# A transformer kernel: the engines' orders, the PSUM banks and the splitting of maxima are changed

## The chip, the cores and the metric

The kernel runs on one core of a Trainium2 chip. The metric is device time in microseconds (us) from the start to the end of one execution; the runs of the kernel before took 1797.16 to 1802.51 us, with a median of 1798.53 us. A core has five engines that run side by side, each through its own instructions in a fixed order: TensorE (PE, matrix products into PSUM), VectorE (DVE), ScalarE (ACT), GpSimd (POOL) and SyncE (SP, which here only starts DMAs). An instruction that needs another engine's result waits for a semaphore, and what stands behind it on its engine waits too. PSUM has eight banks, each of which holds 512 float32 values on each of 128 partitions.

## The reference

The input x has 16 sequences of 512 tokens with 128 values. Two layers follow each other, all in float32:

```python
x = x + attn0(layernorm(x))   # 16 heads of 8, softmax(q k^T / sqrt(8)) v, output projection
x = x + ffn0(layernorm(x))    # silu(x Wg) * (x Wu), then Wd; 384 hidden values, integer weights / 127
x = x + attn1(layernorm(x))   # as attn0, with q and k normalised per head (rms_norm) and weighted
x = x + ffn1(layernorm(x))    # base_w, plus 8 low-rank experts weighted by a softmax router
```

The softmax subtracts each row's maximum before the exponential, and so does the kernel. For each sequence and layer there are 16 heads x 512 queries x 512 keys of scores.

## The kernel before

One sequence in one layer is a unit; there are 32 units, and `units` lists them so that a sequence's second layer comes at least six units after its first (LAG). A unit has four phases.

- `pre(n)`: layer norm (bn_stats on DVE, the rest on POOL), transposes on PE, projections to q and k. `split_stack` (L205) writes each of q and k as a sum of three bf16 parts (ACT and POOL) and starts 24 DMAs on SP (L232) that stack the parts into `qst` and `kst`, so that one bf16 matmul of about 61 rows gives a score of float32 precision. Three sets of these stacks exist (NST).
- Maxima: `max_tile` (L336) multiplies for 128 queries and 512 keys (L343); DVE reduces the 512 columns to the negative maximum (L350). Two heads use the upper and lower 64 rows of PE and run together as a pair. After half a unit `split_max` (L354) splits the maxima into three bf16 parts on DVE, and `put_max` (L363) brings them through PE (L368) and ACT (L376) and with two DMAs on ACT's queue (L378) into three more rows of `qst`. The next product then has its row maximum subtracted.
- Exponentials and values: a step is one (n, i, kc); there are 16 in a unit, 512 in all. `exp_pair` makes two pairs of transposed scores in a step (L395) and ACT takes their exponentials (L403). `values` (L405) multiplies four heads at once by v and a column of ones (L415), in one PSUM bank of its own. After four steps ACT copies the bank (L425) and starts a DMA to DRAM (L427).
- `gather(n)` fetches the sums and the denominators from DRAM in another layout (L452 to L458), and `post(n)` has the output projection and the feed-forward part.

Everything but the values takes its PSUM bank from one pool `psw` of seven banks that go round. The order of PE and POOL is written out by hand: `attend(s)` issues one step after `ORDER = "0mmvmm1b"` (a pair of scores, a pair of maxima, values, a pair of maxima, a pair of scores, other work), and the generators `pre`, `gather` and `post` are advanced at fixed steps after the tables PRE, POST and GATHER (`plan`, `agenda`). The maxima run LEAD = 13 steps ahead of the exponentials. DVE, ACT and SP are ordered by the framework's own scheduler.

Of the kernel before, what the change touches and what calls it, by code (L numbers as in the profile page):

```python
# [17 lines left out]
DRAM = bass.MemoryType.DRAM  # L18

P = 128  # L20
S = 512
# [9 lines left out]
LOWEST = -3.4028234e38  # L31
# [13 lines left out]


LAG = 6
LEAD = 13
LEAD0 = 13
PUT = 2  # L50
ORDER = "0mmvmm1b"
PRE = (
    (-4, 4, 8, 20, 21, 21),
    (1, 2, 4, 6, 7, 9, 9, 12, 12, 12, 14, 20, 21, 22),
)
POST = (
    (5, 7, 9, 10, 11, 12, 13, 15, 15, 16, 17, 17, 17, 17),
    (5, 7, 8, 8, 9, 11, 12, 13),
)
GATHER = (1, 1, 3)  # L60
# [3 lines left out]
BO0, BQK1, BP1, BB1, RB1, REND = 0, 128, 384, 512, 640, 648  # L64


@with_exitstack
def encoder_kernel(ctx: ExitStack, tc: tile.TileContext, x, wf, wi, lb, cols, rows, out):
# [4 lines left out]
    xp = ctx.enter_context(tc.tile_pool(name="xp", bufs=LAG + 3))  # L73
    p1 = ctx.enter_context(tc.tile_pool(name="p1", bufs=1))
    p2 = ctx.enter_context(tc.tile_pool(name="p2", bufs=2))
    pp = ctx.enter_context(tc.tile_pool(name="pp", bufs=3))
    dr = ctx.enter_context(tc.tile_pool(name="dr", bufs=2, space=DRAM))
    psw = ctx.enter_context(tc.tile_pool(name="psw", bufs=7, space=PSUM))
    psa = ctx.enter_context(tc.tile_pool(name="psa", bufs=1, space=PSUM))

    xt_of = {}

    def load_x(b):
        xt = xp.tile([P, C, P], F32, tag="xt", name=f"xt{b}")
        nc.sync.dma_start(xt, x[b].rearrange("(c p) d -> p c d", p=P))
        xt_of[b] = xt
# [29 lines left out]
    def fill(i):  # L116

        eng = nc.vector if i == 0 else nc.gpsimd
        eng.memset(kst[i].rearrange("p t s -> p (t s)").bitcast(F32), ONES)
        eng.memset(vst[i], 1.0)  # L120

    def fill_q(i):

        q = qst[i].rearrange("p t s -> p (t s)").bitcast(F32)
        if i == 0:
            nc.scalar.activation(q, zero[:, None, :].to_broadcast([P, 4, S]), AF.Copy)
        else:
            nc.gpsimd.memset(q, 0.0)

    def weights():  # L130

        for layer, (lo, bb) in enumerate(((WO0, BO0), (WP1, BP1))):
            bvb = p1.tile([P, P], F32, tag="bvb", name=f"bvb{layer}")
            nc.vector.tensor_scalar(bvb, zero[:, :P], cl[:, 4 + layer : 5 + layer], None, ALU.add)
            ps = psw.tile([P, P], F32, tag="w", name=f"bvp{layer}")
            nc.tensor.matmul(ps, bvb, w[:, lo : lo + P], start=True, stop=True)
            nc.vector.tensor_tensor(row[:, bb : bb + P], row[:, bb : bb + P], ps, ALU.add)
            yield
        nc.vector.tensor_copy(identb, ident)
        nc.vector.tensor_scalar(b2, b2, 2.0, None, ALU.mult)  # L140
        nc.vector.tensor_scalar(qkn, cl[:, 2:4], math.sqrt(HD), None, ALU.mult)
        yield
        for k in range(3):
            wint = p1.tile([P, HID], I32, tag="wint", name=f"wint{k}")
            nc.scalar.dma_start(wint, wi[:, k * HID : (k + 1) * HID])
            if k < 2:
                nc.vector.tensor_copy(wgu[:, k * HID : (k + 1) * HID], wint)
            else:
                nc.vector.tensor_scalar(
                    wd.rearrange("p f o -> p (f o)"), wint, 0.5 / 127.0**3, None, ALU.mult  # L150
                )
            yield

    fill(0)
    fill_q(0)
# [9 lines left out]
    )  # L165
    av_last = [None]

    av_of, nm_of, num_of, mp_of, p_of, acc_of = ({} for _ in range(6))

    def layer_norm(xt, nm, alone=False):  # L170
        st = p2.tile([P, C, 6], F32, tag="st", name=f"st{nm}")
# [621 lines left out]
```

## Time and profile before

| | |
|---|---|
| profiled execution, its time | 1800.01 us |
| its span, first to last instruction | 1798.0 us |
| median of three runs | 1798.53 us |
| mean granted TensorE clock | 0.976 |
| POOL busy | 753.8 us (42%) |
| SP: stack DMAs issued | 768, 64 KB each, 0.61 us of SP for most |
| ACT: DMAs issued | 127 of 256 KB (0.33 us each), 128 of 12 KB (0.73 us each) |

How to read what follows: a row of a group gives line, engine, operation, output<-input, shapes and the count; then the busy time in us and the mean of one in ns; then the idle time of the engine just before these instructions and what ended most of it. Matmuls are pipelined: a row of 0.39 us for a pair doesn't mean that the next pair starts 0.39 us later, so the distance between the starts is used here. A float32 matmul is recorded twice. In a timeline the columns are start and duration in us, and brackets show the idle time before. In a tile view the columns are the shortest, median and longest duration in ns and the first and last start in us.

### The profile page before, as it was taken

Reading aid. Unit: us, or ns where it says so; the run is one execution under the profiler, and the core shown is the slowest. Engines: PE = TensorE matmul, PEld = TensorE weight load, DVE = VectorE, ACT = ScalarE, POOL = GpSimd, SP = SyncE. Lnnn points to the kernel's source line nnn. Section 1 sums busy time; section 2 is a strip of 40 time slices with the busy share of each in tenths; the row PEclk is TensorE's granted clock in tenths of the full one; section 3 lists DMA queues with packets and bytes.
Section 4 is the critical chain, followed back from the end, with each engine's and each line's share of the span. In section 5 each row is a group of like instructions: output and inputs, shape, how many; then the busy total and the mean of one; then the engine's idle time right before and its main releaser. Section 6 shows DMA issues by size and latency. Waiting matters only on the chain.

```text
span 1798.0 us, 30523 instructions
## 1 busy us (share of the span) xinstructions
PE 1676.6 (93%) x10574; PEld 552.3 (31%) x10574; DVE 1577.7 (88%) x3234; ACT 1346.7 (75%) x2578; POOL 753.8 (42%) x853
## 2 busy tenths in 40 slices
PE   4899999999999999999999999999999999998996
PEld 1223233322323223233323323323232333332323
DVE  6888989899898998989899998989998999998973
ACT  2388868878787777878878787887877877787783
POOL 4223345344354345345345444434445555454111
PEclk7699999999999999999999999999999999999997
DMA  5332232232332223233232342323233123333110
GB/s 124 41 73 63 60 67 50 62 62 60 68 75 56 72 62 72 68 67 68 58 71 67 61 82 55 70 63 63 64 74 70 49 68 60 67 73 73 45 45 27
DMA packets 111658, 115.85 MB, mean 64 GB/s; under 512 B 19300, under 2 KB 86852, under 8 KB 111504
## 3 DMA queue, kind: packets, MB, share of 16 engines
q1 hardware_dynamic: 90612, 77.64, 23.4%
q10 hardware_dynamic: 20892, 36.26, 5.7%
q8 instruction: 83, 1.36, 0.3%
q14 instruction: 71, 0.58, 0.1%
HBM read 23.43 MB, written 38.53 MB: 34 GB/s over the span
## 4 chain that ended last, share of the span: by engine, by line
PE 55%; DVE 27%; DMA 11%; ACT 2%; issue 2%; SPq 1%; POOL 1%; ACTq 0%; POOLq 0%; DVEq 0%
PE avp L415 19%; DVE nm L350 19%; PE s L343 11%; PE st L395 6%; DMA qst<-a10a 4%; PE u_f L513 3%; PE g_f L507 3%; PE d_f L526 2%; ACT p L403 2%; PE r_f L589 1%; PE r_f L588 1%; PE o L480 1%; DMA dav<-av 1%; PE pm L368 1%; DMA kst<-a31a 1%
## 5 line engine op out<-in xcount | busy, mean ns | idle before, releaser
L350 DVE TENSOR_REDUCE nm<-s 128x1 f32<-128x512 f32 x2048 | 1296.4, 681 | 148.8 <-PE s L343 141.2
L403 ACT ACTIVATE p<-st 128x512 f32<-128x512 f32 x2048 | 1091.9, 599 | 325.3 <-PE st L395 266.3
L415 PE MATMUL avp<-p,vst 128*32 128x512 f32 x4096 | 629.0, 606 | 21.3 <-ACT p L403 21.3
L343 PE MATMUL s<-kst,qst 61*128 61x512 bf16 x2048 | 490.7, 388 | 56.2 <-DVE nm L350 20.8
L395 PE MATMUL st<-qst,kst 64*128 64x512 bf16 x2048 | 371.9, 381 | 2.1 <-DMA qst<-msb 2.0
L343 PEld LDWEIGHTS <-qst 61*128 61x128 bf16 x2048 | 115.9, 94 | 508.3 <-issue 479.0
L415 PEld LDWEIGHTS avp<-p,vst 128*32 128x32 f32 x4096 | 112.0, 108 | 367.1 <-issue 234.4
L460 POOL TENSOR_TENSOR num<-num,rdb 128x512 f32<-128x512 f32 x31 | 39.5, 1273 | 306.2 <-DMA rdb<-drd 306.2
L395 PEld LDWEIGHTS <-kst 64*128 64x128 bf16 x2048 | 104.8, 95 | 136.1 <-issue 94.8
L519 POOL TENSOR_TENSOR h_f<-th_f,ub_f 128x512 f32<-128x512 f32 x32 | 40.9, 1277 | 237.8 <-ACT ub_f L518 237.8
L220 POOL TENSOR_TENSOR t1a<-t1a,a11a 128x512 f32<-128x512 f32 x31 | 36.0, 1162 | 161.5 <-ACT a11a L214 116.1
L425 ACT ACTIVATE av<-avp 128x512 f32<-128x512 f32 x128 | 76.5, 598 | 19.3 <-PE avp L415 16.9
L567 POOL TENSOR_TENSOR cf_f<-gt_f,mid_f 128x256 f32<-128x256 bf16 x16 | 9.9, 620 | 128.7 <-DVE gt_f L565 128.7
L201 POOL TENSOR_TENSOR xt<-xt,row 128x512 f32<-128x512 f32 x48 | 61.6, 1283 | 2.7 <-DVE xna L184 1.4
L376 ACT ACTIVATE msb<-pm 24x512 bf16<-24x512 f32 x64 | 36.8, 574 | 29.6 <-PE pm L368 29.6
L513 PE MATMUL u_f<-xTf,wgu 128*128 128x512 f32 x96 | 54.0, 645 | 0.0
L507 PE MATMUL g_f<-xTf,wgu 128*128 128x512 f32 x96 | 52.3, 627 | 0.0
L526 PE MATMUL d_f<-wd,h_f 128*128 128x128 f32 x384 | 47.1, 279 | 0.0
L526 PEld LDWEIGHTS d_f<-wd,h_f 128*128 128x128 f32 x384 | 44.1, 192 | 6.8 <-issue 5.1
L220 POOL TENSOR_TENSOR t0a<-t0a,a10a 128x512 f32<-128x512 f32 x31 | 35.9, 1159 | 16.7 <-ACT a10a L214 13.0
L224 POOL TENSOR_TENSOR a20a<-t0a,zero 128x512 bf16<-128x512 f32 x31 | 39.6, 1277 | 2.4
L297 POOL TENSOR_TENSOR qksa<-qksa,ria 128x512 f32<-128x512 f32 x32 | 40.0, 1271 | 1.2
(140 smaller groups left out, 1633.9 us busy)
## 6 DMA issues: line engine op xcount, KB each, us to landing
dav<-av ACTq DMA_DIRECT2D x127, 256.0 KB
kst<-a11a SPq DMA_DIRECT2D x192, 64.0 KB
qst<-a10a SPq DMA_DIRECT2D x192, 64.0 KB
kst<-a21a SPq DMA_DIRECT2D x128, 64.0 KB
qst<-a20a SPq DMA_DIRECT2D x128, 64.0 KB
num<-dav SPq DMA_DIRECT2D x31, 256.0 KB
rdb<-drd SPq DMA_DIRECT2D x31, 256.0 KB
xt<-in_x_dram SPq DMA_DIRECT2D x16, 256.0 KB
```

The costliest lines, as they stand in the source:

```text
L201: nc.gpsimd.tensor_tensor(xt, xt, row[:, None, lo : lo + P].to_broadcast([P, C, P]), ALU.add)
L220: eng.tensor_tensor(t, t, a1, ALU.subtract)
L343: nc.tensor.matmul(ps, qst[n % NST][band, t, qc * P : (qc + 1) * P], kst[n % NST][band, t], start=True, stop=True,)
L350: nc.vector.tensor_reduce(nm_of[n, hf][:, qc, half, t % 4 : t % 4 + 1], ps, AX.X, ALU.max, negate=True)
L395: nc.tensor.matmul(st[half], kst[n % NST][band, t, kc * P : (kc + 1) * P], qst[n % NST][band, t], start=True, stop=True,)
L403: nc.scalar.activation(p_of[n, i, kc][:, 2 * jp + half], st[half], AF.Exp, scale=SCALE)
L415: nc.tensor.matmul(acc[32 * j : 32 * j + 32], vst[n % NST][:, kc, lo : lo + 32], pt[:, j], start=(kc == 0), stop=(kc == C - 1), tile_posit ...
L425: nc.scalar.activation(av, acc, AF.Copy)
L507: nc.tensor.matmul(pg, wgu[:, f * P : (f + 1) * P], xT, start=True, stop=True)
L513: nc.tensor.matmul(pu, wgu[:, HID + f * P : HID + (f + 1) * P], xT, start=True, stop=True)
L519: nc.gpsimd.tensor_tensor(h[:, f], th, ub, ALU.mult)
L526: nc.tensor.matmul(ps[:, c], h[:, f, c * P : (c + 1) * P], wd[:, f], start=(f == 0), stop=(f == NF - 1),)
```

## The change

- A class `Plan` in the kernel now orders all five engines. Every piece of work is a generator that yields (engine, estimated ns, priority, kind, what it waits for). `Plan.run` keeps one estimated clock per engine, picks the piece that can start first (among those within EPS the one of lowest priority), and adds estimates for the way between engines (START, TAIL). For PE `choose` goes through PATTERN, where m is a pair of maxima, e a pair of scores, v values and w other work. What comes out is a fixed order; at run time the engines still wait for semaphores.
- The eight PSUM banks are allocated once and handed out by `Banks`: three for maxima, three for scores, one for all other work, and one for the values as before. A pair is planned when two banks of its kind are free.
- The splitting of the maxima (four small operations for each half unit) moves from DVE to POOL, inside `put_max`.
- The DMAs of the values (L427) and of the maxima (L378) move from ACT's queue to SP, so SP starts all DMAs. The stack DMAs are ordered by part.
- The exponentials' SBUF tiles are eight of two heads instead of three of four; LEAD is 20, as a priority only; the integer weights are loaded from SP.

The core of the diff:

```diff
-LEAD = 13
-PUT = 2
-ORDER = "0mmvmm1b"
+LEAD = 20
+NP = 8
+VLAG = 2.0
+EPS = {"PE": 40, "ACT": 100, "DVE": 150, "POOL": 100, "SP": 0}
+PATTERN = "mevmew"
+TOL = {"m": 400, "e": 400, "v": 200, "w": 200}
+NB_M, NB_E = 3, 3
...
+START = {"PE": 45, "ACT": 22, "DVE": 22, "POOL": 68, "SP": 25}
+TAIL = {"PE": 185, "ACT": 118, "DVE": 98, "POOL": 20, "SP": 2600}
+SWITCH = 100
+def act(n, ptr=0):
+    return 51 + n / 1.2 + 93 * ptr
+def red(n):
+    return 62 + n / 0.96
...
-    psw = ctx.enter_context(tc.tile_pool(name="psw", bufs=7, space=PSUM))
-    psa = ctx.enter_context(tc.tile_pool(name="psa", bufs=1, space=PSUM))
+    pst = [ps.tile([P, S], F32, tag=f"ps{k}", name=f"ps{k}") for k in range(8)]
+    acc = pst[7]
+    mbanks = Banks(pst[:NB_M])
+    ebanks = Banks(pst[NB_M : NB_M + NB_E])
+    banks = Banks(pst[NB_M + NB_E : 7])
...
+                    pr = 16 * n + 8 * hf + j / 2 - LEAD
+                    waits = [mbanks.two, ("q", n), ("k", n)]
+                    e = yield "PE", 220, pr, "m", waits
...
-        nc.vector.tensor_copy(mp[:, :, :, 0], nm)
-        nc.vector.tensor_tensor(r1, nm, mp[:, :, :, 0], ALU.subtract)
-        nc.vector.tensor_copy(mp[:, :, :, 1], r1)
-        nc.vector.tensor_tensor(mp[:, :, :, 2], r1, mp[:, :, :, 1], ALU.subtract)
+            t = yield "POOL", 310, pr, None, waits
+                nc.gpsimd.tensor_copy(mp[:, :, :, 0], nm)
+                nc.gpsimd.tensor_tensor(r1, nm, mp[:, :, :, 0], ALU.subtract)
+                nc.gpsimd.tensor_copy(mp[:, :, :, 1], r1)
+                nc.gpsimd.tensor_tensor(mp[:, :, :, 2], r1, mp[:, :, :, 1], ALU.subtract)
...
-            nc.scalar.dma_start(
-                Q[half * HP + MROW : (half + 1) * HP, 4 * hf : 4 * hf + 4],
+            e = yield "SP", 60, pr + 1, None, (t,)
+            nc.sync.dma_start(
+                qst[n % NST][half * HP + MROW : (half + 1) * HP, 4 * hf : 4 * hf + 4],
...
-                nc.scalar.dma_start(av_of[n][i], av)
+            e = yield "SP", 60, pr, None, (t,), 800
+            nc.sync.dma_start(av_of[n][i], av)
...
-    with tc.manual_schedule(engines={mybir.EngineType.PE, mybir.EngineType.Pool}):
-        for s in range(min(agenda), max(agenda) + 1):
-            attend(s)
-        flush()
+    plan.spawn(weights())
+    for i in range(1, NST):
+        plan.spawn(fill(i))
+    plan.spawn(scores())
+    plan.spawn(values())
+    plan.spawn(maxima())
+    for n in range(NU):
+        plan.spawn(chain(n))
+    with tc.manual_schedule(engines={ET.PE, ET.Pool, ET.DVE, ET.Activation, ET.SP}):
+        plan.run()
```

In the changed kernel the maxima's matmul is L625, their reduction L640, the splitting L656 to L663, `put_max`'s matmul L669 and its DMAs L682, the scores L704, the exponentials L721, the values L738.

## The prediction, made before the changed kernel had run

> **What bounds the kernel now.** I read the page's engine shares first, then the costliest groups, the waits, two stretches of the timeline, and last the tiles qst and msb.
>
> ```profile
> PE 1676.6 (93%) x10574; PEld 552.3 (31%) x10574; DVE 1577.7 (88%) x3234; ACT 1346.7 (75%) x2578; POOL 753.8 (42%) x853
> ...
> L350 DVE TENSOR_REDUCE nm<-s 128x1 f32<-128x512 f32 x2048 | 1296.4, 681 | 148.8 <-PE s L343 141.2
> L403 ACT ACTIVATE p<-st 128x512 f32<-128x512 f32 x2048 | 1091.9, 599 | 325.3 <-PE st L395 266.3
> ```
>
> Two engines look full, and each waits for the other: VectorE (DVE) has 141.2 us of idle time that a score matmul of the maxima (L343) ended. One step is one (n, i, kc) of the exponentials; there are 512. The tile view of qst and, under it, the timeline of TensorE (PE) give the period and its parts.
>
> ```profile
> L395 PE MATMUL st<-qst,kst x2048: 372/378/632, 70.5 to 1769.0; 64*128 64x512 bf16 x187
> ```
> ```profile
> 900.18 0.39 PE L395 MATMUL st<-qst,kst 64*128 64x512 bf16 x2
> 900.41 0.38 PE L343 MATMUL s<-kst,qst 61*128 61x512 bf16 x2
> 900.72 1.06 PE L415 MATMUL avp<-p,vst 128*32 128x512 f32 x8
> 901.72 0.39 PE L343 MATMUL s<-kst,qst 61*128 61x512 bf16 x2
> 901.94 0.38 PE L395 MATMUL st<-qst,kst 64*128 64x512 bf16 x2
> 902.25 1.13 PE L255 MATMUL qkv1a<-w,xTa 128*128 128x256 f32 x4
> 903.32 0.39 PE L395 MATMUL st<-qst,kst 64*128 64x512 bf16 x2
> ```
>
> Two stretches of a step without other work, PE's rows and then DVE's:
>
> ```profile
> 932.87 0.60 PE L395 MATMUL st<-qst,kst 64*128 64x512 bf16 x4
> 933.30 0.88 PE L343 MATMUL s<-kst,qst 61*128 61x512 bf16 x2
> 934.11 1.35 PE L415 MATMUL avp<-p,vst 128*32 128x512 f32 x8
> 935.40 0.39 PE L343 MATMUL s<-kst,qst 61*128 61x512 bf16 x2
> ```
> ```profile
> 930.30 2.48 DVE L350 TENSOR_REDUCE nm<-s 128x1 f32<-128x512 f32 x4 [0.23 <-PE s L343]
> 933.06 2.48 DVE L350 TENSOR_REDUCE nm<-s 128x1 f32<-128x512 f32 x4 [0.27 <-PE s L343]
> ```
>
> First scores start at 70.5 us and last ones at 1769.0 us: 511 steps of 3.32 us, and 99.5 us at the two ends (70.5 + 29.0). The starts at 900 us are of a step with one piece of other work: PE never stands, and the step takes 3.14 us. A pair of scores costs 0.22 us; a pair before values or other work 0.31, so the change of kind costs 0.09; values cost 1.00 with the change out of them, so 0.91. The step at 933 us has no other work: the second maximum of a pair waits for its bank (0.88 instead of 0.39), PE gives time away, and the step takes as long as DVE's four reductions, 2.76 us from start to start. So the bound alternates from step to step, PE where other work stands, DVE where none does. That, and not one full engine, makes 3.32.
>
> **Work of each engine per step.** PE: four pairs, 4 x 0.223 = 0.89; values 0.91; other work, from starts in the timeline (0.86 for an f32 matmul of 512 columns, 0.43 for 256, 0.22 for 128, 0.11 for a transpose), 12.7 us for a unit of layer 0 and 10.4 for one of layer 1, so 0.72 per step; changes of kind 1649 x 0.088 / 512 = 0.28. Sum 2.80. DVE: 4 x 0.598 = 2.39 (four reductions in 2.48 us, the last one 0.68 long); norms, gates, residuals and squares 6.2 us per unit of layer 0, 8.1 of layer 1, so 0.45; and the splitting of maxima. ScalarE (ACT): exponentials start 0.48 apart when none waits, 1.91 of 3.32. It is no bound.
>
> **The change part by part.**
>
> *Splitting of maxima to GpSimd (POOL).* The four DVE groups L358 to L361 are busy 17.0, 19.9, 22.4 and 11.5 us, 71 us in all; by starts about 0.9 us per half unit, 57 us, 0.11 per step. DVE falls from 2.95 to 2.84. POOL gets 256 small instructions; the nearest rows are L180 (128x4, 230 ns) and L291 (128x128, 455 ns), so 59 to 116 us; I take 80, and its share goes from 42% to about 49%. The four depend on each other, and each may stand behind an instruction of 1.27 us, so the maxima are ready later, not earlier. Here a rule speaks against the change: the Trainium skill, "Perfetto Trace Analysis", Optimizing Scalar/DVE Operations, says GpSimd and VectorE share an SBUF read port, so that moving work between these two might not help. By the trace, the reductions read PSUM and start 0.597 to 0.601 us apart while POOL is 42% busy, so what leaves DVE is won; by the rule the 57 us would shrink. I take the row.
>
> *New order.* In the built instruction order PE has the same 1024 pairs of maxima, 1024 pairs of scores and 512 values. Other work now stands in 477 places instead of 313, so the long stretches without any and the knots of four or five pieces become fewer. Price: 1974 changes of kind instead of 1649, 325 x 0.088 = 29 us of PE, 0.06 per step; PE goes to 2.86. The Trainium skill, "TensorEngine Tiling (Array Packing)", Key Properties, says that a change of tiling mode drains TensorE. Estimated with the drain of about 175 ns that "TensorE: Matmul & The Clock Gate", Single matmul latency, gives, this would be 57 us; the rows 900.18 to 900.72 show 0.09 each, and they decide.
> To see what evenness is worth I laid these durations on both instruction orders, cut after every fourth maximum, and added up the larger of PE's and DVE's work in each cut: 3.20 us per step before, 3.09 after. With cuts of two steps it is 3.14 and 3.03, with half steps 3.25 and 3.23. Measured before is 3.32, so 0.12 is friction.
>
> *Banks.* Before, seven banks go round for all kinds, so a maximum can wait for an exponential's bank. After, three belong to maxima, three to scores, one to all other work, and a pair needs two of three: the next pair can be complete only when the first of the running pair is reduced. Half a step of PE is 1.43 us and a pair's reductions 1.20, so this holds in most steps; a long DVE instruction (msa L271, 1.0) uses the slack up. No row shows a bank of one kind alone, so from both sides: the friction goes (0), or the coupling is as tight as half steps (3.23 - 3.09 = +0.14). I take 0.04 left, nearer to zero, since in the row at 933 us the wait is for a DVE bank while PE has time.
> The single bank: of 451 pieces of other work most have 2.1 us of PE work behind them before the next needs the bank, and free it in 0.7 to 1.4 us (matmul 0.2 and activation 0.5, twice where two engines read). Only put_max and layer 1's transposes of q and k have 0.6 to 0.8 us. At about 0.5 us for 32 of these, 16 us at most, under PE's slack; I take nothing.
>
> *DMA issues from ACT to SP.* ACT loses 127 issues of 0.33 us and 128 of 0.73, 135 us during which exponentials stood behind; as ACT is no bound, the gain is in friction and counted there. SP gets them: 768 x 0.61 + 134 + some 80 = 680 us, 40% of the time, with bursts of 12 stack pieces (12 x 0.61 = 7.3 us) that the scheduler costs at 0.06 each.
>
> ```profile
> L378 ACTq DMA_DIRECT2D qst<-msb x128: 728/729/1367, 64.9 to 1742.1; - x128
> L376 ACT ACTIVATE msb<-pm x64: 570/570/587, 64.3 to 1739.7; 24x512 bf16<-24x512 f32 x64
> ```
>
> A maximum's way from put_max to qst is 0.43 (to ACT's start) + 0.57 + 0.77 (second issue) + about 2.3 (from an issue to its user, as den L452 to L455) = 4.1 us or more. Before, PE has 6.4 to 10.7 us of work between put_max and the first scores that need it. After, in 18 of 64 halves only 2.9 to 3.5 us. Each stands 1.2 us there: 22 us. The stacks: from the last q/k matmul to the last issue takes 16 to 20 us now, with 13 steps (43 us) until the first maximum; after, 4 to 11 steps, which is enough except in four units (6, 7, 8, 27), short by 22 us in all. While PE stands DVE still has up to three tiles, 1.8 us, so half of these 44 us is lost: 22 us.
>
> *Ends.* 22 pairs of maxima stand before the first scores instead of 26, and the last 13 steps have none, as before. I keep 99.5 us.
>
> **Sum.** 99.5 + 511 x (3.09 + 0.04) + 22 = 1721 us of span. The profiled execution took 1800.01 us with a span of 1798.0; the median of the runs is 1798.53, so the span stands for the time: 1720 us.
>
> **Rivals.**
> *Nearly the full balance.* The order was made with durations close to the rows here (0.478 for an exponential, 0.595 for a reduction), so PE and DVE may even out over two steps with no friction and no late data: 99.5 + 511 x 3.03 = 1648 us. For it: DVE needs 2.84 and PE 2.86. Against: three banks hold less than a step.
> *The private banks tie PE to DVE.* Half-step coupling, 3.23, with 0.09 of friction: 99.5 + 511 x 3.32 = 1796 us, no change. For it: other work adds up to 4 or 5 us in some steps and no bank is there to bridge it. Against: the idle PE at 933 us.
> *Maxima arrive late (slower).* Place: the SP queue between the msb issues and the scores L704. All DMAs stand in one queue in a fixed order; behind a burst of stacks, or behind a residual chain that waits for a landing, an msb issue is 2 to 7 us late, PE stands in order, and maxima, values and other work stand behind it. Over 99.5 + 511 x 3.13 = 1699 us there are 99 us until 1798; over 64 halves it decides from 1.55 us lost per half. At 2.2 us it gives 1840 us. For it: 18 halves have less than 3.5 us. Against: most msb issues follow an av issue (0.33 us) and not a stack.
> That the order is not as told can be left out: the instruction order shows it.
>
> **How the numbers follow.** The forecast 0.45 (1670 to 1770 alone), the full balance 0.22, tied banks 0.13 (half of it faster, a quarter within 0.3%), late maxima 0.20. A measurement of this kernel can tell 0.3% from no change, so faster than 1793: 0.45 + 0.22 + 0.07 = 0.74; the same 0.03; slower 0.23. The range goes from 1635, under the full balance, to 1820, which takes in tied banks and part of the late maxima.
>
> **What would show it.** In the profile after: first to last L704 over 511 steps, near 3.16 with late data; DVE busy about 60 us less, no split rows on it, and less idle ended by the maxima's matmul; waits of L704 for msb of some 1 us in about 18 halves; waits of the first L625 of a unit for stacks in few units; ACT without issues. Wrong would be: PE's waits for msb over 100 us in sum, the second maximum of pairs waiting in most steps, or other work waiting for its bank by more than 50 us.

## The result, and the profile after

The changed kernel takes 1885.61 us (median of 4 runs, 1883.99 to 1888.02) against 1797.85 us (median of 4) for the kernel before in the same session: a ratio of 1.0484, 95% interval 1.0462 to 1.0507. It is slower by 88 us; the forecast was 1720 us. The profiled execution has a span of 1882.1 us and a mean granted clock of 0.966.

The page of the changed kernel, lines for the engine shares, PE and its clock in 40 slices, and the groups that answer to those shown of before:

```profile
PE 1674.0 (89%) x10574; PEld 530.6 (28%) x10574; DVE 1542.9 (82%) x2978; ACT 1359.6 (72%) x2578; POOL 809.5 (43%) x1109
...
PE   3597699978979999989999999999999979999886
...
PEclk9998899989989999999999999999999999999997
...
L640 DVE TENSOR_REDUCE nm<-ps 128x1 f32<-128x512 f32 x2048 | 1288.1, 683 | 197.2 <-PE ps L625 188.0
L721 ACT ACTIVATE p<-ps 128x512 f32<-128x512 f32 x2048 | 1104.5, 596 | 368.3 <-PE ps L704 365.2
L625 PE MATMUL ps<-kst,qst 61*128 61x512 bf16 x2048 | 481.2, 394 | 109.7 <-DVE nm L640 61.3
...
L704 PE MATMUL ps<-qst,kst 64*128 64x512 bf16 x2048 | 455.3, 385 | 28.3 <-DMA qst<-msb 23.4
...
L656 POOL CAST mp<-nm 128x32 bf16<-128x32 f32 x64 | 13.4, 209 | 281.0 <-DVE nm L640 281.0
```

The same lines of the page of before:

```profile
PE   4899999999999999999999999999999999998996
...
L343 PE MATMUL s<-kst,qst 61*128 61x512 bf16 x2048 | 490.7, 388 | 56.2 <-DVE nm L350 20.8
L395 PE MATMUL st<-qst,kst 64*128 64x512 bf16 x2048 | 371.9, 381 | 2.1 <-DMA qst<-msb 2.0
```

The work is the same and DVE has less of it, but PE, DVE and ACT all wait more. PE's idle time before the maxima (L625) is 109.7 us where it was 56.2 (L343), and before the scores 28.3 where it was 2.1. The slices tell where: PE's 5 to 8 tenths lie in the first third. POOL stands 281 us in order at the first of the four splitting instructions (L656), for maxima that are not reduced yet. The tile view of qst gives the first and last scores:

```profile
L704 PE MATMUL ps<-qst,kst x2048: 372/377/631, 98.2 to 1851.0; 64*128 64x512 bf16 x187
```

Cut by the first scores of each unit, the 84.1 us between the two spans are: the start 27.7 (98.2 instead of 70.5), units 0 to 7 57.0 (487.0 instead of 430.0), units 8 to 30 -3.7 (1220.8 instead of 1224.5), the last unit and the end 3.0. So the loss lies at the start and in the first eight units. Idle stretches of PE over 1.5 us, counted from its first matmul on, add up to 119.6 us, against 41.7.

One of them in three views. SP's queue (each row is a group of DMA issues), then DVE, then PE:

```profile
145.43 4.27 SPq L462 DMA_DIRECT2D kst<-a11a  x6
149.79 2.57 SPq L462 DMA_DIRECT2D kst<-a21a  x4
152.47 0.61 SPq L462 DMA_DIRECT2D kst<-a31a  x1
...
154.28 3.87 SPq L462 DMA_DIRECT2D qst<-a10a  x6
158.26 2.57 SPq L462 DMA_DIRECT2D qst<-a20a  x4
160.93 1.26 SPq L462 DMA_DIRECT2D qst<-a30a  x2
162.27 0.61 SPq L802 DMA_DIRECT2D den<-dav  x1
```
```profile
154.62 1.88 DVE L640 TENSOR_REDUCE nm<-ps 128x1 f32<-128x512 f32 x3
168.15 0.55 DVE L807 RECIPROCAL den<-den 128x64 f32<-128x64 f32 x1 [11.65 <-DMA den<-dav]
```
```profile
156.85 0.38 PE L625 MATMUL ps<-kst,qst 61*128 61x512 bf16 x1
169.30 0.58 PE L625 MATMUL ps<-kst,qst 61*128 61x512 bf16 x1 [12.08 <-DVE nm L640]
...
170.24 1.93 PE L738 MATMUL ps<-p,vst 128*32 128x512 f32 x8
...
177.17 1.07 PE L738 MATMUL ps<-p,vst 128*32 128x512 f32 x8
```

The scheduler booked 24 stack pieces at 24 x 0.06 = 1.4 us; they take 16.8 us of SP, with one DMA of the values between them. The fetch of the denominators (L802) stands behind them, its data come 5.9 us after its issue (2.1 to 2.6 before, in 30 of 31 units), and DVE stands 11.65 us in order at the reciprocal (L807), which the plan had put ahead of the next reductions. No maximum's bank comes free, so PE stands for 12.08 us, with the releaser "DVE nm" in its row; the cause is two engines further back. After the gap the same eight matmuls of the values take 1.93 us, and 1.07 a little later. The view by stretches (columns: busy time of PE, PE's weight loads, DVE, ACT, POOL, then granted clock, DMA share, GB/s) shows why:

```profile
145.00:157.00 12.00, 10.96 (x77) 3.23 (x74) 10.03 (x16) 9.42 (x18) 0.00 (x0) 1.00 0.47 88
157.00:169.20 12.20, 0.23 (x3) 0.00 (x0) 1.05 (x3) 1.08 (x2) 0.00 (x0) 0.60 0.56 89
169.20:176.50 7.30, 6.69 (x32) 1.19 (x32) 5.59 (x13) 4.22 (x8) 1.28 (x1) 0.74 0.37 112
176.50:190.00 13.50, 13.29 (x93) 3.86 (x92) 13.18 (x33) 11.98 (x25) 6.08 (x11) 1.00 0.06 23
```

The clock falls in the gap and stays down some microseconds after it. So this gap is paid for twice. Over the execution the clock is at a half in 13 stretches of 130.9 us together, before in 6 of 88.3 us; the last one of each kernel runs on some 2 us past its last instruction.

### The profile page after: what moved, and what is told of

It reads as the page before. It is cut to its first block, busy times and chain, and to the rows that moved or that the text cites. A ratio compares the mean times of both kernels' runs of the same rounds, so it can differ in the third digit from the quotient of the medians.

```text
span 1882.1 us, 30801 instructions
## 1 busy us (share of the span) xinstructions
PE 1674.0 (89%) x10574; PEld 530.6 (28%) x10574; DVE 1542.9 (82%) x2978; ACT 1359.6 (72%) x2578; POOL 809.5 (43%) x1109
## 4 chain that ended last, share of the span: by engine, by line
PE 57%; DVE 19%; DMA 11%; ACT 6%; issue 3%; POOL 2%; SPq 2%; ACTq 0%; POOLq 0%; DVEq 0%
PE ps L738 18%; DVE nm L640 13%; PE ps L625 13%; PE ps L704 8%; ACT p L721 3%; DMA qst<-msb 3%; PE ps L919 3%; DMA qst<-a10a 2%; PE ps L892 2%; PE ps L882 2%; SPq L462 2%; DMA kst<-a21a 2%; PE ps L591 1%; PE ps L572 1%; PE ps L1005 1%
## 5 line engine op out<-in xcount | busy, mean ns | idle before, releaser
L640 DVE TENSOR_REDUCE nm<-ps 128x1 f32<-128x512 f32 x2048 | 1288.1, 683 | 197.2 <-PE ps L625 188.0
L721 ACT ACTIVATE p<-ps 128x512 f32<-128x512 f32 x2048 | 1104.5, 596 | 368.3 <-PE ps L704 365.2
L625 PE MATMUL ps<-kst,qst 61*128 61x512 bf16 x2048 | 481.2, 394 | 109.7 <-DVE nm L640 61.3
L738 PE MATMUL ps<-p,vst 128*32 128x512 f32 x4096 | 570.0, 615 | 0.6 <-ACT av L755 0.4
L704 PE MATMUL ps<-qst,kst 64*128 64x512 bf16 x2048 | 455.3, 385 | 28.3 <-DMA qst<-msb 23.4
L625 PEld LDWEIGHTS <-qst 61*128 61x128 bf16 x2048 | 105.2, 93 | 635.8 <-issue 598.5
L738 PEld LDWEIGHTS ps<-p,vst 128*32 128x32 f32 x4096 | 89.1, 109 | 229.9 <-issue 219.3
L704 PEld LDWEIGHTS <-kst 64*128 64x128 bf16 x2048 | 105.1, 95 | 162.7 <-issue 118.8
L656 POOL CAST mp<-nm 128x32 bf16<-128x32 f32 x64 | 13.4, 209 | 281.0 <-DVE nm L640 281.0
L755 ACT ACTIVATE av<-ps 128x512 f32<-128x512 f32 x128 | 76.7, 599 | 21.5 <-PE ps L738 20.8
L919 PE MATMUL ps<-wd,h_f 128*128 128x128 f32 x384 | 61.2, 297 | 0.3 <-DVE h_f L906 0.3
L892 PE MATMUL ps<-xTf,wgu 128*128 128x512 f32 x96 | 54.0, 645 | 3.8 <-DVE th_f L886 3.8
L919 PEld LDWEIGHTS ps<-wd,h_f 128*128 128x128 f32 x384 | 48.9, 195 | 28.4 <-issue 27.4
L882 PE MATMUL ps<-xTf,wgu 128*128 128x512 f32 x96 | 55.0, 655 | 0.7
L572 PE MATMUL ps<-xTa,w 128*128 128x512 f32 x64 | 41.7, 738 | 6.5 <-DVE xt L928 2.0
```

Source lines behind the costliest of these rows:

```text
L572: nc.tensor.matmul(pt, w[:, lo : lo + P], xT, start=True, stop=True)
L625: nc.tensor.matmul(pair[half][1], qst[n % NST][band, t, qc * P : (qc + 1) * P], kst[n % NST][band, t], start=True, stop=True,)
L640: nc.vector.tensor_reduce(nm[:, qc, half, t % 4 : t % 4 + 1], pt, AX.X, ALU.max, negate=True)
L704: nc.tensor.matmul(pair[half][1], kst[n % NST][band, t, kc * P : (kc + 1) * P], qst[n % NST][band, t], start=True, stop=True,)
L721: nc.scalar.activation(pt[:, half], st, AF.Exp, scale=SCALE)
L738: nc.tensor.matmul(acc[32 * j : 32 * j + 32], vst[n % NST][:, kc, lo : lo + 32], p_of[n, i, kc, j // 2][0][:, j % 2], start=(kc == 0), sto ...
```

## The experiments

My theory after the result: the order is a fixed one, made with wrong estimates (an issue on SP at 0.06 us, the first x at 9 us), and engines that stand in order behind late data lose the time. Rivals: SP as the one queue for all DMAs is the loss, whatever was estimated; the split on POOL makes the maxima late; the three bank groups tie PE to DVE and ACT. Line numbers of the scheduled kernels are those of the changed kernel. The medians of "before" are 1794.9 to 1800.3 us in all sessions.

| run | changed from | median us | ratio to before, 95% interval |
|---|---|---|---|
| e1_dma_cost | after | 1830.56 | 1.0169 (1.0143 to 1.0194) |
| e2_act_queue | after | 2049.25 | 1.1394 (1.1371 to 1.1417) |
| e3_before_split_pool | before | 1965.42 | 1.0930 (1.0903 to 1.0957) |
| e4_before_own_banks | before | 1861.79 | 1.0351 (1.0330 to 1.0372) |
| e5_unit0_first | e1 | 1815.27 | 1.0114 (1.0097 to 1.0131) |
| e6_split_on_dve | e5 | 1886.41 | 1.0514 (1.0498 to 1.0530) |
| e7_banks_4_2_1 | e5 | 1966.19 | 1.0959 (1.0936 to 1.0981) |
| e8_banks_3_2_2 | e5 | 1875.54 | 1.0449 (1.0425 to 1.0472) |
| e9_reductions_yield | e5 | 1786.73 | 0.9934 (0.9909 to 0.9958) |
| e10_unit0_banks | e9 | 1785.34 | 0.9938 (0.9909 to 0.9967) |
| e11_act_queue_costs | e1 | 1915.35 | 1.0672 (1.0619 to 1.0726) |
| e12_shared_banks | e5 | 1793.03 | 0.9966 (0.9947 to 0.9984) |
| e13_shared_later_landing | e12 | 1750.06 | 0.9733 (0.9703 to 0.9764) |
| e14_split_later_landing | e9 | 1800.06 | 1.0014 (0.9999 to 1.0029) |
| e15_after_shared_only | after | 1946.56 | 1.0824 (1.0781 to 1.0867) |

Every run but e3 and e4 is a wholly new order of all five engines, so a difference between two runs holds some luck of the order besides the part that was changed. e14 gives its size: it is 13 us slower than e9 after an edit that was expected to cost 6 us at most. Differences under some 15 us prove little here.

**e1_dma_cost.** Each issue on SP is booked at its measured length (13 lines; two of them):

```diff
-            e = yield "SP", 60, pr(0.1), None, (avail[which], ("stack", n), ("fill", n % NST))
+            e = yield "SP", 652, pr(0.1), None, (avail[which], ("stack", n), ("fill", n % NST))
...
-            e = yield "SP", 60, pr + 1, None, (t,)
+            e = yield "SP", 785, pr + 1, None, (t,)
```

> The changed kernel with one thing altered: the scheduler now costs a DMA's issue on SP at what the trace shows (stack piece 0.652 us, maxima 0.785, values 0.443, den and num 0.633, rdb 0.674, drd 0.430, x 0.505, out 0.482) instead of 0.06 each. The instructions are the same, only their order differs. Theory A (the order is made as if SP were free; stacks, denominators and maxima come late and PE and DVE stand in order behind them): the 46 us of PE gaps before the first maximum of a unit, the 32 us behind the reciprocal of den and a good part of the 27.7 us at the start go; 1770 to 1815 us. Theory B (one queue for all DMAs is simply too much): the load on SP is the same, so under 20 us are won, 1865 to 1890 us. Theory C (three, three and one bank tie the engines together): no gain, 1875 to 1895 us.

1830.56 us: 55 of the 88 us are gone by estimates alone; the computation, the banks and the queues are those of the changed kernel. From the page:

```profile
PE   3598999999899999999999999999999999999986
...
L625 PE MATMUL ps<-kst,qst 61*128 61x512 bf16 x2048 | 489.3, 393 | 60.6 <-DVE nm L640 38.3
L704 PE MATMUL ps<-qst,kst 64*128 64x512 bf16 x2048 | 448.2, 381 | 11.2 <-ACT p L721 6.0
```

By the spans 52.0 of these 55 us are won in units 0 to 7 (435.0 us instead of 487.0): between 100 and 600 us the idle stretches of PE over 1.5 us fall from 59.2 to 11.0 us. Units 9 to 24 take 3.19 us a step, against 3.27. First scores are still at 96.2 us, so theory A's range is missed by 16 us; theories B and C are further off. Wrong costs are the largest part of the loss. The scheduler's own clock tells the same from the other side: it ends 52 us later than the changed kernel's (1709 instead of 1657 us), and the kernel 55 us earlier. A plan that looks worse, with true costs in it, ran faster.

**e2_act_queue.** The DMAs of maxima and values go back to ACT's queue (those of the values with a priority two steps higher), SP's costs stay at 0.06. Of the edit, the part on the maxima:

```diff
-            e = yield "SP", 60, pr + 1, None, (t,)
-            nc.sync.dma_start(
+            e = yield "ACT", 760, pr + 1, None, (t,), 2482
+            nc.scalar.dma_start(
```

> The changed kernel with the DMAs of the maxima and of the values put back on ACT's queue (costed there at 0.76 and 0.37 us); SP's other issues are still costed at 0.06 us. Theory A: the stacks' bursts and den behind them are still ordered as if they were free, so at most the waits of scores for the maxima (21 us of gaps over 1.5 us) go and ACT pays 135 us of issuing: 1850 to 1890 us. Theory B: SP loses 141 of 709 us of issuing and the kernel gains most of what it lost, 1790 to 1840 us. Theory C: 1875 to 1895 us.

2049.25 us, 159 us and more outside all three ranges. SP has less to issue and yet the kernel is much slower, so the load of SP's queue by itself is not the cause. Among PE's waits are late stacks (57.4 us before L625) and late numerators (52.9 us before L835). Why it is 164 us slower than the changed kernel is not shown beyond that.

**e3_before_split_pool.** The kernel before, with its hand-written order, and `split_max` on POOL (four lines; the first):

```diff
-        nc.vector.tensor_copy(mp[:, :, :, 0], nm)
+        nc.gpsimd.tensor_copy(mp[:, :, :, 0], nm)
```

> The kernel before with one part of the change alone: the four splitting operations of the maxima on POOL instead of DVE, at the same places of the order. By the reckoning of the prediction DVE loses 57 us of work, which shows where DVE is the bound: 1765 to 1798 us. If the dependent operations behind POOL's long ones bring the maxima late (5 steps of lead), scores wait for them and it is slower: 1800 to 1840 us. Theory D (the moved splitting is the cause of the loss) needs 1840 us or more.

1965.42 us. The page of e3 has the likely reason in one row:

```profile
L358 POOL CAST mp<-nm 128x32 bf16<-128x32 f32 x64 | 13.3, 208 | 530.5 <-DVE nm L350 530.5
```

POOL stands 530.5 us in order at its first splitting instruction, with all its other work behind it, and PE waits 37.1 us for the splitting before `put_max`'s matmul (L368), where it waited 10.4. What the four instructions cost (13.3 us for the first group) says nothing about what their place costs. In this order the rival has what it asked for, 1840 us or more; e6 puts the same question to an order that was made for the splitting on POOL.

**e4_before_own_banks.** The kernel before with three banks for maxima and four for the rest; `max_tile` takes its tile from `psm`.

```diff
-    psw = ctx.enter_context(tc.tile_pool(name="psw", bufs=7, space=PSUM))
+    psm = ctx.enter_context(tc.tile_pool(name="psm", bufs=3, space=PSUM))
+    psw = ctx.enter_context(tc.tile_pool(name="psw", bufs=4, space=PSUM))
```

> The kernel before with three PSUM banks for maxima alone and four for scores and other work, nothing else altered. Theory C (banks of their own tie PE to DVE): the second maximum of a pair waits more often, 1830 us or more. Theory A: the split of the banks is not what costs, within 15 us of 1798 us.

1861.79 us, 3.44 us a step, as theory C wants it. From 600 to 1700 us the second maxima of pairs start 107 us late in sum (distance of the two starts less the 0.004 us of an undisturbed pair), against 77 us before. Three own banks cost the hand-written order some 62 us.

**e5_unit0_first.** As e1; the scheduler expects the first x at 5 us, so that it no longer puts the second unit's work ahead of the first's.

```diff
-    at.update({"w": 10000, "row": 9500, ("xt", 0, 0): 9000})
+    at.update({"w": 10000, "row": 9500, ("xt", 0, 0): 5000})
```

> The kernel of the run with SP's measured costs, and besides the scheduler is told that sequence 0 lands at 5 us instead of 9, so that unit 0's stacks are issued before unit 1's. Same instructions. Theory A (the ends: first scores came at 96 to 98 us instead of 70.5 because SP issued unit 1's 24 stack pieces first, 24 x 0.652 = 15.6 us, and PE stood in order behind units 1 and 2): first scores near 72 us and 1830 - 25 = 1805 us, 1797 to 1812. If the late start has another cause (the order of the memsets, the weights' DMAs on SP), first scores stay over 90 us and the time over 1822 us.

1815.27 us; first scores at 84.6 us instead of 96.2, half of the way to the 72 us of theory A, and the time is 3 us above its range. The profiled spans of e1 and e5 differ by less (1826.9 and 1823.3): the profiled execution of e5 is its slowest (1825.05 us, the other four 1814.46 to 1816.70), and its unit 26 is longer (83.6 against 78.9 us).

**e6_split_on_dve.** As e5, splitting back on DVE (and the four instructions with it).

```diff
-            t = yield "POOL", 310, pr, None, waits
+            t = yield "DVE", 130, pr, None, waits
```

> As the run with unit 0 first, but the splitting of the maxima is back on DVE (costed at 0.13 us an operation). Theory D1 (the splitting on POOL makes POOL stand in order for DVE, 322 us of it in the run with SP's costs, and its stack work comes late): faster than with unit 0 first alone, by 10 to 40 us. Theory A of the prediction (DVE wins 57 us by the move): slower by 15 to 50 us.

1886.41 us, 71 us slower than e5, where 15 to 50 were expected. In an order that knows of it, the move to POOL is a gain. How large is not clean: e6 books the four operations of a half unit at 0.52 us, 33 us in all, and by the starts in its trace they take 113 us of DVE, so e6 has a wrong cost of its own. Part of the reason stands in the last section.

**e7_banks_4_2_1, e8_banks_3_2_2.** As e5, other shares of the banks.

```diff
-NB_M, NB_E = 3, 3
+NB_M, NB_E = 4, 2
```

> As the run with unit 0 first, with four PSUM banks for maxima, two for scores and one for other work. Theory C (three banks tie PE to DVE: 71 us of waiting inside pairs of maxima between 600 and 1700 us): that waiting falls under 40 us and the kernel wins 10 to 40 us, unless two banks for scores cost as much; then the waiting moves to the scores (ACT) and the time is within 10 us or slower. Theory A: no gain over 10 us.

> As the run with unit 0 first, with three PSUM banks for maxima, two for scores and two for other work. If the single bank for other work holds PE up (20 us of waits between scores and other work from 600 to 1700 us in the run with SP's costs), 10 to 20 us are won; if two banks for scores are too few, scores wait for ACT and it is 10 to 60 us slower. Theory A expects no gain over 10 us.

1966.19 and 1875.54 us. With four banks for maxima the waits inside pairs of maxima fall (69 to 49 us from 600 to 1700, not under 40 as theory C wants), but two banks for scores wait for ACT: the second scores of pairs start 76 and 71 us late in the same stretch instead of 35, and PE's idle time before L704 that ACT ended is 38.1 and 18.0 us over the execution instead of 5.7. A second bank for other work doesn't make up for that. These waits are less than the 151 us that e7 loses; the rest was not traced. Of the fixed splits that I tried, three, three and one is the best.

**e9_reductions_yield.** e5's unit 26 takes 83.6 us, and the scheduler's own clock gives it 72.3. So the hole is planned, and the trace of e5 (DVE, then PE) tells by what:

```profile
1508.44 1.07 DVE L525 TENSOR_REDUCE msa<-sq0a 128x64 f32<-128x512 f32 x1
1509.44 18.09 DVE L640 TENSOR_REDUCE nm<-ps 128x1 f32<-128x512 f32 x30
1527.45 0.68 DVE L886 SCALAR_TENSOR_TENSOR th_f<-th_f,ps 128x512 f32<-128x512 f32 x1
```
```profile
1507.32 1.12 PE L882 MATMUL ps<-xTf,wgu 128*128 128x512 f32 x2
...
1510.47 1.06 PE L738 MATMUL ps<-p,vst 128*32 128x512 f32 x8
...
1516.82 10.75 PE L625 MATMUL ps<-kst,qst 61*128 61x512 bf16 x18 [0.23 <-DVE nm L640]
1528.18 0.59 PE L669 MATMUL ps<-identb,mp 128*24 128x128 bf16 x4 [0.61 <-POOL r L658]
```

L882 takes the one bank of other work at 1507.3. DVE's L886 would give it back, but 30 reductions of a better priority go first. `put_max` (L669) of the next unit needs that bank and comes at 1528.2, so no scores can go on, and with none of them the reductions are almost all that DVE finds.

```diff
-            e = yield "DVE", red(S), pr, None, (e0,)
+            e = yield "DVE", red(S), pr + 4, None, (e0,)
```

> As e5_unit0_first, and the reductions of the maxima stand four steps lower in VectorE's priority (pr + 4), so that an operation of VectorE which frees the single bank of other work is no longer passed over by reductions that run ahead. Theory (the single bank is held by a piece of other work whose VectorE step is starved, put_max waits for that bank, and the scores wait for put_max): the hole at the end of unit 26 (83.6 us for that unit in e5) shrinks to about 51 to 54 us and the time falls by 25 to 32 us, to 1783 to 1790 us. Rival (the lead of the maxima is used up there because VectorE has too much work): the hole stays or comes back in another unit and the time stays within 10 us of 1815 us.

1786.73 us, 28.5 us less; unit 26 takes 57.7 us instead of 83.6 (51 to 54 expected), and DVE's L886 has two reductions ahead of it instead of 30. The theory of the held bank holds, and this kernel is faster than before by 0.7%.

**e10_unit0_banks.** As e9, the first unit's matrix products in the scores' banks, the bias rows and the loads of integer weights after the first stacks. Of the edit:

```diff
+        bk = ebanks if n == 0 else banks
...
-                t = yield "PE", 880, pr(), "w", (tT, banks.one, r_qk if g == 0 else 0.0)
+                t = yield "PE", 880, pr(), "w", (tT, bk.one, r_qk if g == 0 else 0.0)
```

> As e9_reductions_yield, and the first unit's matrix products take the scores' banks, which are free at the start, and the small products for the bias rows and the loads of the integer weights come after the first stacks. Theory (at the start the single bank puts the first projections one behind the other, 1.4 us each time, and the weights' loads and casts stand ahead of the first stacks): first maxima at 36 to 40 us instead of 45.8, first scores at 72 to 78 us instead of 84.6, the time 7 to 12 us below e9's, 1772 to 1783 us. Rival (the 24 stack DMAs and their landing set the start): first scores stay within 3 us of 84.6 and so does the time within 3 us of e9's.

First scores at 76.6 us instead of 84.8, as expected; of these 8.2 us the profiled spans keep 5.1 (1783.6 and 1788.7), and the medians 1.4, which the intervals don't tell from nothing; 7 to 12 were expected.

**e11_act_queue_costs.** e2's queues, by the same edit, with e1's costs.

> As e1_dma_cost (measured cost of each DMA issue in the scheduler), and the DMAs of maxima and values are issued by ScalarE as in the kernel before, with the measured cost of an issue there too (0.76 and 0.37 us). If the place of these DMAs mattered by itself (255 issues that stand behind stacks on SP), this is below e1's 1830.6 us, about 1800 us. If only the wrong estimate mattered and ScalarE's 135 us of issues are now missing to exponentials, it is above e1: 1860 to 1900 us.

1915.35 us, 85 us above e1 and 15 above the second range. With the costs right in both, SP is the better place for these DMAs. That ACT's issues push exponentials back shows in PE's wait for ACT before the scores (27.4 us, 6.0 in e1), which is a quarter of the 85 us; the rest was not traced.

**e12_shared_banks.** As e5, all kinds take their banks from one pool of seven.

```diff
-    mbanks = Banks(pst[:NB_M])
-    ebanks = Banks(pst[NB_M : NB_M + NB_E])
-    banks = Banks(pst[NB_M + NB_E : 7])
+    mbanks = Banks(pst[:7])
+    ebanks = mbanks
+    banks = mbanks
```

> As e5_unit0_first (first kernel of that order: measured issue costs, unit 0 first, reductions not yielding), but the scheduler gives all kinds of work their banks from one pool of seven, as the kernel before has it; a pair still waits for two free banks. Its own clock ends at 1628 us, against 1682 us with three, three and one. Theory (the split is a cost: the single bank's inversion in unit 26 and the coupling of a pair to two of three banks): the gain of the plan arrives, 1750 to 1775 us, with no hole at unit 26 and steady units at 50 us. Rival (the split buys evenness: with shared banks a maximum waits for an exponential's bank as in the kernel before, where an order's error spreads from one kind to the other): steady units at 52 to 54 us, 1790 to 1825 us, and PE's idle time before L704 that ScalarE ends is over 30 us.

1793.03 us. The plan is 54 us shorter, 22 of them arrive. There is no hole at unit 26, but ten gaps over 1.5 us wait for stacks at L625, and the clock is at a half for 149.8 us. Neither expectation is right as it stands: waits for ACT before the scores are few (3.1 us), and the largest wait left at L625 is for late stacks (39.0 us).

**e13_shared_later_landing, e14_split_later_landing.** The scheduler lets stacks land 2 us later, in e12 and in e9.

```diff
-            e = yield "SP", 652, pr(0.1), None, (avail[which], ("stack", n), ("fill", n % NST))
+            e = yield "SP", 652, pr(0.1), None, (avail[which], ("stack", n), ("fill", n % NST)), 2000
```

> As e12_shared_banks, and the scheduler expects a stack DMA to land 2.0 us later than before (4.6 us after its issue instead of 2.6), so that the first maxima of a unit are put behind it. The scheduler's own clock ends at 1628 us as for e12. Theory (e12's lost time is stacks that land later than assumed, with the half clock behind each gap; the shared banks themselves are no worse): gaps before L625 that a30a ends fall from nine to at most three, and the time falls by 20 to 40 us, to 1753 to 1773 us. Rival (the shared banks let an error of one kind of work reach the other kinds, whatever the landing): the time stays within 8 us of e12's 1793 us and other waits stand where the stacks' were.

> As e9_reductions_yield (banks three, three and one, reductions yielding), with the same later landing of stacks as e13. Its own clock ends at 1659 us, against 1654 for e9. If the bank split bridges such errors, this stays within 6 us of e9's 1786.7 us, since e9 has only three gaps of stacks and these cost some 15 us with their half clock. Against e13 it tells what the split costs when stacks are not late: by the two clocks 31 us.

1750.06 us, the fastest kernel of this study, 2.7% below before; three such gaps are left after the start. Page of e13:

```profile
PE 1636.4 (94%) x10574; PEld 532.6 (30%) x10574; DVE 1526.0 (87%) x2978; ACT 1349.2 (77%) x2578; POOL 811.0 (46%) x1109
...
PE   2899999999999999999999999999999899999996
PEclk7799999999999999999999999999999999999997
...
L625 PE MATMUL ps<-kst,qst 61*128 61x512 bf16 x2048 | 431.5, 389 | 44.4 <-DMA qst<-a30a 30.3
```

PE is full from the third slice to the end, and no reduction stands any more at the head of what L625 waits for. The time is 3 us better than the range. Still, the scheduler's own clock ends at 1628 us here, so 122 us of the span are not in the plan.

e14 stays at 1800.06 us, so the later landing is no gain there; it is 13 us above e9, more than I allowed. Its unit 7 alone takes 66.5 us against 55.0, with a gap of 5.0 us before a stack and 6.8 us of half clock; why that stack is late I can't say.

e13 and e14 differ by 50.0 us, in the banks and in the yielding of e9, which was not tried with shared banks. By the spans' 48.2 us: 12.4 at the start (first scores 73.0 and 85.4), 27.2 in units 0 to 7, 0.7 in units 8 to 30, 11.7 in the last unit, less 3.8 at the end. From 600 to 1700 us the waits inside pairs of maxima are 22 us with shared banks and 59 with three of their own, but the 50 us don't come from there: units 8 to 30 take 1201.8 and 1202.5 us. In these units PE's idle time before the maxima is 1.6 us for reductions and 13.3 for stacks with shared banks, 18.2 and 1.8 with own ones: what one kernel loses to reductions the other loses to stacks.

**e15_after_shared_only.** The changed kernel with the bank split alone undone, by the same edit as e12.

> The changed kernel with one part undone: the scheduler hands out all banks from one pool of seven, and keeps its wrong costs (0.06 us for an issue on SP, 9.0 us for the first x). Its own clock ends at 1648 us, against 1657 for the changed kernel. If the bank split costs some 50 us whatever the order's errors, as between e13 and e14, the time is 1820 to 1850 us. If the order's errors on SP set the time and hide the banks, it is 1870 us or more, as the errors of both add up or replace each other.

1946.56 us: 61 us slower than the changed kernel. Its page:

```profile
L625 PE MATMUL ps<-kst,qst 61*128 61x512 bf16 x2048 | 448.9, 398 | 116.8 <-DMA qst<-a30a 93.1
```

The two don't add up, they change sign: with wrong costs the split saves 61 us, with the issues booked right it costs 22 us (e5 to e12), with the landing later besides 50. With shared banks the plan is tighter and relies more on its costs; late stacks then cost 93.1 us at L625, and 26 stretches of half clock come to 268.9 us.

## Why the prediction was wrong, point by point

**What bounds the kernel.** Nearly right where nothing is late: the undisturbed units of the changed kernel take 48.6 to 51 us, 3.04 to 3.19 a step, beside a forecast of 3.13, and units 9 to 24 of e1, all together, take 3.19 (3.35 before). But a step over the whole execution is (1851.0 - 98.2) / 511 = 3.43 us. Evenness was there to be had; the changed kernel didn't reach it. The price of the changes of kind (29 us) wasn't tried by itself.

**Splitting to POOL.** The direction was right, the sizes were put too high: POOL's busy time rises by 55.7 us (80 forecast, 59 at the lower end), four rows of 71 us leave DVE, whose busy time falls by 35 (60 forecast; it counts overlapping durations once). e6 against e5 confirms a gain. The step took the wrong row against the rule on the shared port, though. The row of the reductions shows only that these don't wait for POOL. The splitting itself does (last section): in the kernel before its four rows are drawn out by 25 us in this way, and the prediction passed over it. So the two engines do get into each other's way here, and the move took the splitting out of it; the gain did not shrink for that. That its sign came out right is in part luck. That POOL, in order, would stand 281 us for unreduced maxima was not in the step; e3 shows what that costs where the order doesn't foresee it.

**Banks.** "I take 0.04 left, nearer to zero" failed, and so did "I take nothing" for the single bank. With right issue costs and later landings the split costs about 50 us (e13 to e14). The rival of tied banks has its mechanism in the trace, PE waiting for reductions (18.2 against 1.6 us in units 8 to 30), but most of the 50 us lies at the start, in units 0 to 7 and in the last unit, and by what path is open. The single bank cost 28 us in e5, by a path that I hadn't looked for: not the time of its own turn, but a holder that the scheduler passes over. In the changed kernel itself the split is not what made the loss, since undoing it costs 61 us more (e15).

**DMA issues: the step that failed.** I had 0.61 us of SP for an issue against a booked 0.06, summed it to 680 us (709 measured), and then looked only at maxima (22 us) and at the slack of stacks (22 us), of which half would be lost: "22 us". The 0.55 us that are missing for each of 768 stack pieces are an error of the whole plan: 13.2 us a unit. The runs show 55 us for the wrong issue costs (after to e1), two and a half times the term, and nearly all of it in units 0 to 7. Waits for maxima at L704, on which the forecast and the rival of late maxima rested, are only 23.4 us, so the named sign of being wrong, over 100 us of them, did not show. PE stands 38.8 us for stacks, and DVE 36.0 us at its reciprocal (L807), which I never listed as an instruction behind which reductions wait. And the loss per gap was taken as the gap less DVE's three tiles; at 157 us it is the gap and the half clock behind it. The time from a stack's issue to its landing was a second wrong estimate: booking 2 us more brings 43 us with shared banks (e12 to e13), and nothing with the split (e9 to e14).

The Trainium skill, "TensorE: Matmul & The Clock Gate", Part 1: The HAM clock gate, says that after an idle window of about 3.4 us TensorE goes to half rate until it was busy for about as long, and that the cost is the throttled time times one half. The records here agree with the length: every stretch but the last one of a kernel is 3.41 us or a multiple of it. They don't agree with an idle window of that length: at 157 us the half clock begins 2.1 us after PE stops, in e9 1.0 us after. By that page's one half the 42.6 us more of half clock than before are an estimated 21 us at most. It would have been a reason to count gaps instead of late halves.

**Ends.** "I keep 99.5 us" failed: they are 98.2 + 31.1 = 129.3 us. The number of pairs of maxima ahead of the first scores was right (22 forecast, 21 in the trace), but not when the first pair starts: 69.9 us instead of 34.2, since PE and SP take up the second unit first. e5 takes 11.6 us of that back, e10 8.2 more.

**Sum and rivals.** In the 511 steps a gain of 77 us was forecast (1698.5 less 1599 and 22) and a loss of 54 came (1752.8); the ends add 29.8. Of the 166 us between forecast and result the runs give back 136 in this order: issue costs 55 (e1), the first x 15 (e5), shared banks 22 (e12), later landing 43 (e13). In another order the parts would differ, as e15 shows; the last 30 us are open. The rival of late maxima (1840 us) came nearest: SP's queue was its place, and the mechanism, engines in order behind late data, is what happened, but its victim was mostly not the maximum. The full balance (1648 us) was not seen in any run; e13's 1750 is the best.

## What to carry to other kernels

An order that is fixed before the run is only as good as its smallest estimates: check each against a row of a trace, the issues of DMAs first. Then compare the order's own clock with the measured start of each stage; where the two part most is where to look. The changed kernel takes 11.1 us more than its plan in each of units 0 to 7, and 4.1 in each of units 8 to 30. Here sharing the banks made the plan shorter and more sensitive to its errors, so mend the errors before judging how to share. Where a resource of one is held, ask which queued instruction gives it back, and what may be put ahead of that instruction.

## What the runs showed of the hardware

- A gap of 1.9 us can be enough for the half clock. In e9, PE is full up to 1467 us, stands for 1.92 us, and then runs 6 us at a clock of 0.51 (same columns as above). Another gap of e9, of 1.84 us at 565.7, brought none. In before, after and e9 the half clock always begins a whole multiple of 3.413 us after the stretch before it, so where a gap falls may decide; that was not tried.

```profile
1460.00:1467.00 7.00, 6.91 (x42) 3.29 (x40) 6.38 (x12) 4.10 (x8) 3.76 (x8) 1.00 0.62 84
1467.00:1469.00 2.00, 0.08 (x2) 0.04 (x1) 0.69 (x1) 0.00 (x0) 1.64 (x6) 0.76 0.44 81
1469.00:1475.00 6.00, 6.00 (x28) 1.18 (x32) 3.40 (x6) 3.58 (x7) 5.16 (x8) 0.51 0.47 137
```

- The clock also fell without a long gap, while PE had little to do: in e5 it is at a half for 20.5 us from 1516.8; from 1512.6 us up to there PE makes only one maximum in each 0.6 us, with 0.37 us of work and 0.23 us of idle time.
- An issue's time on SP does not go by its bytes: 0.61 us for a stack piece of 64 KB, 0.76 for a maximum's 12 KB, 0.33 for a 256 KB tile of the values.
- A small DVE operation can wait for POOL. In the kernel before, the 184 splitting operations without POOL beside them take at most 0.20 us. All 56 that start more than 0.06 us before the end of a running POOL operation end after it; 42 take 0.3 to 1.26 us and end 0.03 to 0.05 us behind it. DVE, then POOL:

```profile
993.45 1.26 DVE L359 TENSOR_TENSOR r<-nm,mp 128x32 f32<-128x32 f32 x1
...
995.92 0.18 DVE L361 TENSOR_TENSOR mp<-r,mp 128x32 bf16<-128x32 f32 x1
```
```profile
993.40 1.26 POOL L460 TENSOR_TENSOR num<-num,rdb 128x512 f32<-128x512 f32 x1 [6.54 <-DMA rdb<-drd]
```

DVE's reductions, which read PSUM, take 0.681 us in the median with POOL beside them or without. In e6, 46 of the 256 splitting operations are drawn out in this way, up to 1.29 us, which is part of the 113 us there.
